# Second-layer sums of one batch moved from VectorE to GpSimd, and the third layer's first loads issued by GpSimd

## The chip, the cores and the metric

The kernel runs on one core of a Trainium2 chip. The metric is the time on the device in microseconds. TensorE is called PE, VectorE DVE, ScalarE ACT, GpSimd POOL, and SyncE, which issues most DMAs, SP.

## What is computed

The input x is 2 x 256 x 64 x 64 in float32 and passes through four layers:

```python
# layer 0: attention
xn = group_norm(x);  q, k, v = split(einsum(xn, w_qkv))        # 4 heads of 64, 4096 pixels
x = xn + w_proj @ (softmax(q k^T / 8) v) + b_proj
# layer 1: x = x + pe, a fixed position term
# layer 2: bottleneck with a deformable 3x3 convolution on 64 channels
h = relu(bn1(w1 @ x))
off = conv3x3(h, woff) + boff                                  # 9 x (dy, dx) and 9 masks
samp = bilinear(h, base + off) * sigmoid(mask)                 # four corners, weighed and summed
x = relu(bn3(w3 @ relu(bn2(einsum(samp, w2) + b2))) + x)
# layer 3: twice group norm, relu, deformable 3x3 convolution on 256 channels
f = depthwise7x7(h, dw);  off = pw @ f + pwb                   # offsets
h = einsum(bilinear(h, base + off), w) + b
out = h + x
```

## The kernel before

**Order.** `attention` (layers 0 and 1, and most of layer 2 in its background) is followed by `deform` (layer 3, with the second batch's layer-2 convolution in its background). PE, ACT, DVE and POOL execute in the order in which the program issues their instructions; the order of SP's DMAs is left to the scheduler of the framework.

**Attention.** There are four units (batch, pair of heads), each of 16 blocks of 256 queries, each of 16 score tiles of 128 x 1024. The loop takes two tiles at a time, a pair: PE makes scores (L538), DVE their maxima (L547), ACT the exponentials (L554), PE transposes them (L566), DVE or ACT copies the transposes (L581, L583), and PE multiplies by the values (L593). DVE copies the product to `o` (L432). At the end of a block the factors of its parts go through DRAM (`share_d`) into `f`, and POOL combines (L477, L478, L483, in some blocks L485); seven slots later PE projects (L502).

**Background.** Beside its own planned steps, a pair has up to three slots in which generators do a step each. The first batch's `before` (image of h, offsets, corners) runs beside unit 1, its `conv` beside units 2 and 3, then `early_image`, which writes the normalized result to DRAM `xn_d[0]`. The second batch's `before` ends after the last block.

**The convolution of layer 2.** `conv` has 144 steps a batch. A step gathers two corner tiles of 128 x 256 by indirect DMA from POOL (L775), four steps ahead in attention; DVE weighs them by the corner weights in place (L956, "weigh"); one background step later it adds corners pairwise (L965) and once more (L966, "add"), which gives two sampled taps. Four such sums form a group, which PE transposes (L976) after the next sum has been issued, or at once for the last group; there are 40 groups. PE then multiplies (L985, L994). The gather buffers (`bfour`) are five in attention, nine in `deform`.

**Memory.** Tile pools lie in SBUF in the order in which they are opened. In `attention`, `att_w`, `att_work` and `att_one` are opened first, so they lie lowest; `att_one` holds `o`, `f`, `res`, `avs` and others that are used until attention's last instructions. In `deform` the pool `df_w` is opened first, over the same addresses; it holds `x0` (32 KB a partition), `wide0`, `wide1`, `dw`, `pw`, `wf` and nine weights `wc0` to `wc8`.

**The start of layer 3.** `load(0, ...)` reads `xn_d[0]` into `x0` by four DMAs of 1 MB on SP (L1122); POOL clears `wide` (L1127); `offset_weights` reads `dw` and `pw` on SP (L1133, L1135) and DVE makes `wf` of them (L1140); nine `wc` are loaded on SP (L1154). PE then computes offsets (L735, L752, L766), DVE their corners (L680 to L718), and POOL gathers (`four`, L775). `Side` makes a generator keep a rate of steps; before the main loop, 58 rounds advance the first offsets by two steps and the second batch's `conv` by one in every three rounds:

```python
offs = [Side(-LEAD - 6, OFFS / BLOCK, offsets(0, 0))]
for k in range(K2):
    conv_weight(0, k)
for s in range(-LEAD - 6, 0):
    offs[0].follow(s + 1)
    if s % 3 == 0:
        next(second)
```

Of the kernel before, what the change touches and what calls it, by code (L numbers as in the profile page):

```python
# [9 lines left out]
F32 = mybir.dt.float32  # L10
# [8 lines left out]
P = 128  # L19
B, C, H, W = 2, 256, 64, 64  # L20
# [5 lines left out]
DWK = 7  # L26
# [12 lines left out]
class Net:  # L39
# [108 lines left out]
    def attention(self, bott):  # L148
# [4 lines left out]
        tc, nc, a = self.tc, self.nc, self.a  # L153
        with ExitStack() as ctx:
            wp = ctx.enter_context(tc.tile_pool(name="att_w", bufs=1))
            work = ctx.enter_context(tc.tile_pool(name="att_work", bufs=2))
            one = ctx.enter_context(tc.tile_pool(name="att_one", bufs=1))
            xp = ctx.enter_context(tc.tile_pool(name="att_x", bufs=4))
            qp = ctx.enter_context(tc.tile_pool(name="att_q", bufs=2))
            kp = ctx.enter_context(tc.tile_pool(name="att_k", bufs=5))  # L160
            vp = ctx.enter_context(tc.tile_pool(name="att_v", bufs=6))
            ep = ctx.enter_context(tc.tile_pool(name="att_e", bufs=4))
            etp = ctx.enter_context(tc.tile_pool(name="att_et", bufs=2))
            bt = bott.pools(ctx)
            psc = ctx.enter_context(tc.tile_pool(name="att_sc", bufs=2, space=PSUM))
            ptp = ctx.enter_context(tc.tile_pool(name="att_tt", bufs=2, space=PSUM))
# [30 lines left out]
            for i in range(NB):  # L197
                t = xp.tile([P, 2, 512], F32, name="xb") if i < 4 else rest[:, i - 4]
# [8 lines left out]
            gmask = wp.tile([P, P], F32, name="gmask")  # L207
            nc.sync.dma_start(gmask, a["gmask"][:, 0, :])
            nc.sync.dma_start(wqkv, a["wqkv"])
            wproj = wp.tile([P, 2, C], F32, name="wproj")  # L210
            self.later.append((wproj, a["wproj"]))

            units = [(b, hp) for b in range(B) for hp in range(2)]
# [415 lines left out]
            n = 0  # L629
# [153 lines left out]
    class Bottleneck:  # L783
# [148 lines left out]
        def conv(self, b, pools, ps):  # L932
            net, nc = self.net, self.net.nc
            s, t = net.bn_s, net.bn_t
# [15 lines left out]
            def weigh(n):  # L950

                i, g, js = steps[n]
                four, ks = fours.pop(n), self.GROUPS[g]
                w = self.w4[b, i]
                w = w[:, js[0], ks[0] : ks[0] + 2, :] if g < 4 else w[:, js[0] : js[0] + 2, ks[0], :]
                nc.vector.tensor_tensor(  # L956
                    four, four, w.unsqueeze(3).to_broadcast([P, 2, 4, CM]), ALU.mult
                )
                return four

            def add(n, four, sampled):

                i, g, js = steps[n]
                sm = pools["s"].tile([P, 2, CM], F32, name="bsmp")
                nc.vector.tensor_add(four[:, :, 0:2, :], four[:, :, 0:2, :], four[:, :, 2:4, :])  # L965
                nc.vector.tensor_add(sm, four[:, :, 0, :], four[:, :, 1, :])  # L966
                if g < 4:
                    sampled.append(sm.rearrange("p n f -> p (n f)"))
                else:
                    sampled.extend(sm[:, m, :] for m in range(2))  # L970
# [41 lines left out]
            for n, (i, g, js) in enumerate(steps):  # L1012
                gather(n + ahead)
                if g == 0 and js == (0,):
                    x = self.block(pools["x"], net.xa_d[b], i)
                four = weigh(n)
                yield "b"
                add(n, four, sampled)
                if last:
                    last.popleft()()  # L1020
# [63 lines left out]
    def deform(self, bott):  # L1084
# [4 lines left out]
        tc, nc, a = self.tc, self.nc, self.a  # L1089
        with ExitStack() as ctx:  # L1090
            wp = ctx.enter_context(tc.tile_pool(name="df_w", bufs=1))
            work = ctx.enter_context(tc.tile_pool(name="df_work", bufs=2))
# [22 lines left out]
            x, stats = {}, dict(bott.stats)  # L1115

            def load(b, src, pool):
                x[b] = pool.tile([P, 2, HW], F32, name=f"x{b}")
                src = src.rearrange("(cb p) n -> p cb n", p=P)
                for i in range(4):  # L1120
                    cols = slice(1024 * i, 1024 * i + 1024)
                    nc.sync.dma_start(x[b][:, :, cols], src[:, :, cols])  # L1122

            load(0, self.xn_d[0], wp)
            ods = [wp.tile([P, 8, W + DWK - 1], F32, name=f"wide{n}") for n in range(2)]
            for t in ods:
                nc.gpsimd.memset(t, 0.0)  # L1127
            base = bott.base

            def offset_weights(l):  # L1130

                dw = wp.tile([P, 2, T], F32, name="dw")
                nc.sync.dma_start(dw, a["dw"][l])  # L1133
                pw = wp.tile([P, 2, 2 * K2], F32, name="pw")
                nc.sync.dma_start(pw, a["pw"][l])  # L1135
                yield
                yield
                self.wf = wp.tile([P, 2, T, 2 * K2], F32, name="wf")
                for cb in range(2):
                    nc.vector.tensor_tensor(  # L1140
                        self.wf[:, cb],
                        dw[:, cb].unsqueeze(2).to_broadcast([P, T, 2 * K2]),
                        pw[:, cb].unsqueeze(1).to_broadcast([P, T, 2 * K2]),
                        ALU.mult,
                    )
                    yield
# [9 lines left out]
            def image(b, l):  # L1156

                if l == 0:
                    load(b, self.x2d[b], ctx.enter_context(tc.tile_pool(name="df_x1", bufs=1)))
# [39 lines left out]
            def offsets(b, l):  # L1199
                if b == 0:  # L1200
                    yield from offset_weights(l)
                wf = self.wf
                for i in range(NB):
                    idx = cp.tile([P, 4, K2], I32, name="didx")
                    w4 = cp.tile([P, 4, K2, 4], F32, name="dw4")
                    corners[b, l, i] = idx, w4
                    yield from self.offsets(
                        i,
                        [x[b][:, cb, :] for cb in range(2)],
                        lambda s, row: wf[:, s, DWK * row : DWK * row + DWK, :].rearrange(  # L1210
                            "p t o -> p (t o)"
                        ),
                        self.vec[:, V_PWB + l : V_PWB + l + 1],
                        base, idx, w4, work, ods, pd,
                    )

            layers = [(b, l) for l in range(2) for b in range(B)]
            BLOCK = 4 * K2
            LAYER, ALL = NB * BLOCK, len(layers) * NB * BLOCK
            AHEAD, LEAD = 8, BLOCK + 16  # L1220
# [119 lines left out]
            OFFS = 24  # L1340
            inner = ExitStack()
            second = bott.conv(1, bott.pools(inner, 9), ps)
            offs = [Side(-LEAD - 6, OFFS / BLOCK, offsets(0, 0))]
            for k in range(K2):
                conv_weight(0, k)
            for s in range(-LEAD - 6, 0):
# [10 lines left out]
            for s in range(ALL + 12):  # L1357
                n = s // LAYER
# [22 lines left out]
                if s % LAYER == LAYER - LEAD - 8 and n + 1 < len(layers):  # L1381
                    for o in images + offs:
                        for _ in o.steps or ():
                            pass
                    images, offs = [], []
                    offs.append(Side(s, OFFS / BLOCK, offsets(*layers[n + 1])))
# [97 lines left out]
```

## Time and profile before

| what | value |
|---|---|
| median of 3 runs | 5523.4 us (5519.6 to 5540.4) |
| profiled execution | 5528.8 us, span 5527.0 us |
| PE busy | 4928.5 us (89%) |
| DVE busy | 4232.0 us (77%) |
| ACT busy | 2888.5 us (52%) |
| POOL busy | 2069.2 us (37%) |
| POOL's DMA queue | 679.59 MB; SP's 234.46 MB |

Attention ends at about 3100 us of the span, the second batch's `conv` at about 3900 us, and the third layer fills the rest. A line of the timeline gives start, length, engine, program line, operation, tile written and tile read; a number in square brackets is how long the engine had been idle, and behind it what released it. "SPq" and "POOLq" are the sequencers that issue DMAs. A group's line gives the count, then busy us and mean ns, then idle us before and their releasers. Issue instructions are not counted as busy time.

### The profile page before, as it was taken

To read this page: it belongs to the slowest core of one execution; us is meant where nothing else is said; L and a number is where in the kernel's file an instruction comes from. 1 tells how busy PE (TensorE), PEld (TensorE's weight loads), DVE (VectorE), ACT (ScalarE), POOL (GpSimd) and SP (SyncE) were. 2 spreads that over 40 slices of the span, in tenths; PEclk is the share of its full clock that TensorE was granted. 3 is DMA by queue.
4 is the path that set the end of the run, shared out by engine and by line. 5 is a ranking of instruction groups with operands and counts; after the bars stand their busy time and mean duration, and the time that the engine had idled before them with its cause. 6 is when DMAs were issued, how large, how long until landed. Compare 5 with 4: busy or idle time off the path is not lost.

```text
span 5527.0 us, 99087 instructions
## 1 busy us (share of the span) xinstructions
PE 4928.5 (89%) x37976; PEld 2677.3 (48%) x37976; DVE 4232.0 (77%) x8066; ACT 2888.5 (52%) x5333; POOL 2069.2 (37%) x1947
## 2 busy tenths in 40 slices
PE   8999999999999998999899746555899999999998
PEld 5555555555555555555555322222444444444443
DVE  6878767777588787578566366657798989999998
ACT  5676656666566666566667312122444444444444
POOL 0111110100034333232000266656466556656665
PEclk9999999999999999999999878777999999999999
DMA  5231111111222222222411366655999999999998
GB/s 164 65 93 47 51 57 49 34 43 34 63 68 83 86 83 83 85 70 61 132 46 28 108 209 198 186 182 187 330 322 331 329 333 348 345 389 349 337 349 305
DMA packets 347369, 920.38 MB, mean 167 GB/s; under 512 B 58972, under 2 KB 98698, under 8 KB 346894
## 3 DMA queue, kind: packets, MB, share of 16 engines
q0 software_dynamic: 193536, 679.59, 35.4%
q1 hardware_dynamic: 153358, 234.46, 13.8%
q8 instruction: 298, 4.88, 0.4%
q14 instruction: 177, 1.45, 0.1%
HBM read 815.90 MB, written 89.60 MB: 164 GB/s over the span
## 4 chain that ended last, share of the span: by engine, by line
PE 64%; DVE 16%; issue 8%; ACT 6%; another core or an unknown queue 4%; DMA 1%; POOL 1%; ACTq 0%; SPq 0%; DVEq 0%; POOLq 0%
PE av L593 14%; PE sc L538 14%; PE out L1285 10%; PE tt L566 9%; DVE smp L1254 8%; PE pd L735 5%; PE pt L1266 3%; DVE low L547 2%; ACT e L554 2%; DVE bfour L956 1%; PE pm L985 1%; DVE bfour L965 1%; PE pm L502 1%; PE pm L249 1%
## 5 line engine op out<-in xcount | busy, mean ns | idle before, releaser
L1254 DVE SCALAR_TENSOR_TENSOR smp<-four,dw,smp 128x256 f32<-128x256 f32 x3456 | 1612.1, 483 | 311.2 <-ACT smp L1248 162.8
L554 ACT ACTIVATE e<-sc,low 128x1024 f32<-128x1024 f32 x1024 | 1146.0, 1119 | 734.4 <-DVE low L547 714.1
L775 POOL DMA_INDIRECT four<-img,didx x1152 | 1159.1, 1006 | 738.1 <-DVE smp L1254 299.1
L547 DVE TENSOR_REDUCE low<-sc 128x1 f32<-128x1024 f32 x1024 | 1209.4, 1219 | 282.4 <-PE sc L538 273.2
L1285 PE MATMUL out<-st,wc 128*128 128x512 f32 x2304 | 1238.5, 620 | 199.5 <-ACT st L1275 114.9
L538 PE MATMUL sc<-k,qs 64*128 64x512 f32 x2048 | 1026.4, 620 | 10.1 <-ACT e L554 9.5
L538 PE MATMUL sc<-k,q 64*128 64x512 f32 x2048 | 1015.3, 619 | 0.5 <-issue 0.5
L593 PE MATMUL av<-et,v 128*64 128x256 f32 x8192 | 1005.6, 385 | 0.0
L566 PEld LDWEIGHTS tt<-ident,e 64*128 64x128 f32 x16384 | 662.8, 139 | 582.1 <-issue 287.1
L477 POOL TENSOR_TENSOR o<-o,f 128x1024 f32<-128x1024 f32 x64 | 153.1, 2392 | 1934.2 <-DMA f<-share_d 924.7
L775 POOL DMA_INDIRECT bfour<-img,bidx x576 | 581.3, 1009 | 743.6 <-DVE bsmp L966 545.3
L566 PE MATMUL tt<-ident,e 64*128 64x64 f32 x16384 | 731.2, 227 | 96.0 <-ACT et L583 80.3
L583 ACT COPY et<-tt 128x512 f32<-128x512 f32 x1280 | 722.2, 587 | 105.8 <-PE tt L566 80.3
L1275 ACT COPY st<-pt 128x1024 f32<-128x1024 f32 x288 | 291.3, 1012 | 927.6 <-PE pt L1266 637.3
L593 PEld LDWEIGHTS av<-et,v 128*64 128x64 f32 x8192 | 558.3, 137 | 306.7 <-issue 57.8
L1266 PEld LDWEIGHTS pt<-ident,smp 128*128 128x128 f32 x2304 | 321.1, 145 | 771.8 <-issue 503.2
L581 DVE COPY et<-tt 128x512 f32<-128x512 f32 x768 | 525.2, 684 | 171.6 <-PE tt L566 148.3
L1285 PEld LDWEIGHTS out<-st,wc 128*128 128x128 f32 x2304 | 393.4, 197 | 460.2 <-issue 280.0
L1248 ACT ACTIVATE smp<-four,dw 128x256 f32<-128x256 f32 x1152 | 514.2, 502 | 68.1 <-DMA four<-img,didx 55.9
L1266 PE MATMUL pt<-ident,smp 128*128 128x128 f32 x2304 | 459.5, 282 | 93.1 <-DVE smp L1254 80.6
L538 PEld LDWEIGHTS sc<-k,qs 64*128 64x128 f32 x2048 | 349.0, 191 | 263.3 <-issue 133.7
L735 PE MATMUL pd<-x,wf 128*126 128x512 f32 (+2 forms) x896 | 463.0, 604 | 10.1 <-issue 9.2
(154 smaller groups left out, 3342.5 us busy)
## 6 DMA issues: line engine op xcount, KB each, us to landing
f<-share_d SPq DMA_DIRECT2D x128, 256.0 KB
xb<-xn SPq DMA_DIRECT2D x55, 512.0 KB
img<-imgt SPq DMA_DIRECT2D x96, 256.0 KB
four<-img,didx POOLq DMA_INDIRECT x1152
xa<-res SPq DMA_DIRECT2D x32, 512.0 KB
xb<-in_x SPq DMA_DIRECT2D x20, 512.0 KB
bfour<-img,bidx POOLq DMA_INDIRECT x576
qs<-q SPq DMA_DIRECT2D x64, 128.0 KB
```

What stands on the lines that cost most here:

```text
L538: nc.tensor.matmul(s[:, j, :], lhsT=q[u, i // 2][int(h != j)][halves[j], at : at + P], rhs=k[u][c][halves[j], h, :], start=True, stop=True,)
L547: nc.vector.tensor_reduce(low, s, AX.X, ALU.max, negate=True)
L554: nc.scalar.activation(e.rearrange("p j n -> p (j n)"), s, AF.Exp, bias=blk.low[:, g, c : c + 1], accum_out=blk.sum[:, g, c : c + 1],)
L566: nc.tensor.transpose(pt[:, m, :], e[half, m // 4, m % 4 * P : m % 4 * P + P], self.ident[half, half],)
L581: nc.vector.tensor_copy(dst, pt)
L583: nc.scalar.copy(dst, pt)
L593: nc.tensor.matmul(now["av"][halves[h], :], lhsT=v[u][c][:, m, halves[h]], rhs=ets[j][:, m, h, :], start=(m == 0), stop=(m == 7),)
L735: nc.tensor.matmul(pd[:m, r0 * W : r1 * W], lhsT=wt(s, t), rhs=src[:, (y + r0) * W : (y + r1) * W], start=(n == 0), stop=(n == len(srcs) * ...
L775: self.nc.gpsimd.indirect_dma_start(out=dst, out_offset=None, in_=img, in_offset=bass.IndirectOffsetOnAxis(ap=idx, axis=0),)
L1254: nc.vector.scalar_tensor_tensor(smps[s], four[:, c], weight(s, c), smps[s], ALU.mult, ALU.add)
L1266: nc.tensor.transpose(pts[u][:, c, j * P : (j + 1) * P], smp[:, c * P : c * P + P], self.ident,)
L1285: nc.tensor.matmul(outs[ob], lhsT=wc[k][:, c, ob * P : ob * P + P], rhs=sts[u][:, c, :], start=(k == 0 and c == 0), stop=(k == K2 - 1 and ...
```

## The change

- In `attention` the pools `att_work` and `att_one` are opened after the larger ones and so lie above them; `wproj` moves from `att_w` into `att_one`.
- In `conv`, both adds of the first batch go to POOL; those of the second batch stay on DVE. The weighing stays on DVE for both.
- In `deform`, the loads of x of the first batch, and the first layer's `dw` and `pw`, are issued by POOL and no longer by SP.
- The generator of the first offsets is begun (its first step, the two loads) before x is loaded and `wide` is cleared; `Side` receives it with one step done.

```diff
             wp = ctx.enter_context(tc.tile_pool(name="att_w", bufs=1))
-            work = ctx.enter_context(tc.tile_pool(name="att_work", bufs=2))
-            one = ctx.enter_context(tc.tile_pool(name="att_one", bufs=1))
...
             etp = ctx.enter_context(tc.tile_pool(name="att_et", bufs=2))
+            work = ctx.enter_context(tc.tile_pool(name="att_work", bufs=2))
+            one = ctx.enter_context(tc.tile_pool(name="att_one", bufs=1))
...
-            wproj = wp.tile([P, 2, C], F32, name="wproj")
+            wproj = one.tile([P, 2, C], F32, name="wproj")
...
                 i, g, js = steps[n]
+                engine = (nc.gpsimd, nc.vector)[b]
                 sm = pools["s"].tile([P, 2, CM], F32, name="bsmp")
-                nc.vector.tensor_add(four[:, :, 0:2, :], four[:, :, 0:2, :], four[:, :, 2:4, :])
-                nc.vector.tensor_add(sm, four[:, :, 0, :], four[:, :, 1, :])
+                engine.tensor_add(four[:, :, 0:2, :], four[:, :, 0:2, :], four[:, :, 2:4, :])
+                engine.tensor_add(sm, four[:, :, 0, :], four[:, :, 1, :])
...
-                    nc.sync.dma_start(x[b][:, :, cols], src[:, :, cols])
-
-            load(0, self.xn_d[0], wp)
-            ods = [wp.tile([P, 8, W + DWK - 1], F32, name=f"wide{n}") for n in range(2)]
-            for t in ods:
-                nc.gpsimd.memset(t, 0.0)
+                    queue = (nc.gpsimd, nc.sync)[b]
+                    queue.dma_start(x[b][:, :, cols], src[:, :, cols])
...
+                queue = (nc.gpsimd, nc.sync)[l]
                 dw = wp.tile([P, 2, T], F32, name="dw")
-                nc.sync.dma_start(dw, a["dw"][l])
+                queue.dma_start(dw, a["dw"][l])
                 pw = wp.tile([P, 2, 2 * K2], F32, name="pw")
-                nc.sync.dma_start(pw, a["pw"][l])
+                queue.dma_start(pw, a["pw"][l])
...
+            begun = offsets(0, 0)
+            next(begun)
+            load(0, self.xn_d[0], wp)
+            ods = [wp.tile([P, 8, W + DWK - 1], F32, name=f"wide{n}") for n in range(2)]
+            for t in ods:
+                nc.gpsimd.memset(t, 0.0)
...
-            offs = [Side(-LEAD - 6, OFFS / BLOCK, offsets(0, 0))]
+            offs = [Side(-LEAD - 6, OFFS / BLOCK, begun)]
```

## The prediction

> **What bounds the kernel now.** I read the slices of the page first: PE is 9 tenths busy in the first 22 slices (attention) and the last 12 (third layer), and 5 to 7 tenths between about 3100 and 3900 us. The change touches two places: the first batch's second layer, which runs inside attention, and the handover from attention to the third layer. So I asked for windows. The first row below is attention without this work, the others are attention with it (columns: window, length, then busy us and instructions of PE, PEld, DVE, ACT, POOL, then PE clock, DMA share, GB/s).
>
> ```profile
> 800.00:1440.00 640.00, 632.92 (x6880) 375.68 (x6880) 483.92 (x746) 411.08 (x765) 65.38 (x45) 1.00 0.15 42
> 1612.00:2240.00 628.00, 579.80 (x5923) 336.41 (x5920) 488.67 (x742) 400.23 (x744) 253.92 (x225) 0.98 0.29 84
> 2330.00:2626.00 296.00, 276.05 (x2850) 162.02 (x2850) 235.68 (x370) 197.23 (x369) 97.45 (x88) 0.99 0.25 71
> ```
>
> PE idles 7.1 us of 640 (1.1%) in the first, 48.2 + 20.0 = 68.2 us of 924 (7.4%) in the others. At 1.1% it would idle 10; so **58 us is all that these windows can give back**. In the chain of waits the first window is PE (618 us) with 20 us of ACT; in the other two PE is 572 us and DVE 197, of which the moved sums are 44 (L965 24.3 + 10.5, L966 4.3 + 5.3). The reason: scores feed the maximum (L547, DVE), that feeds the exponential, that feeds PE's transposes; a sum ahead of L547 in DVE's order delays all three. From the groups of instructions, 1580 to 2626 us, the rows concerned:
>
> ```profile
> L547 DVE TENSOR_REDUCE low<-sc 128x1 f32<-128x1024 f32 x328 | 387.8, 1218 | 123.5 <-PE sc L538 118.8 <-remote 2.6 <-PE tt L566 0.2
> L956 DVE TENSOR_TENSOR bfour<-bfour,bw 128x512 f32<-128x512 f32 x144 | 101.8, 707 | 0.4 <-issue 0.4
> L965 DVE TENSOR_TENSOR bfour<-bfour 128x256 f32<-128x256 f32 x144 | 81.5, 566 | 1.7
> L966 DVE TENSOR_TENSOR bsmp<-bfour 128x128 f32<-128x128 f32 x144 | 58.7, 408 | 4.9
> L775 POOL DMA_INDIRECT bfour<-img,bidx x280 | 276.0, 986 | 547.3 <-DVE bsmp L966 485.5 <-issue 49.7 <-DVE lowest L436 6.1
> L477 POOL TENSOR_TENSOR o<-o,f 128x1024 f32<-128x1024 f32 x20 | 49.1, 2455 | 84.1 <-DVE o L432 43.3 <-DVE pos L689 29.4 <-DVE bsmp L966 5.6
> ```
>
> The last two columns are busy and mean, then the idle before. POOL has room: it idles 485 us before gathers, waiting for the sums to free a buffer. The medians of L965 and L966 are 419 and 292 ns, so their means hold 21 + 17 = 38 us of stall. The timeline shows where from:
>
> ```profile
> 1916.12 2.67 POOL L477 TENSOR_TENSOR o<-o,f 128x1024 f32<-128x1024 f32 x1 [3.12 <-DVE o L432]
> 1916.61 2.46 DVE L965 TENSOR_TENSOR bfour<-bfour 128x256 f32<-128x256 f32 x1
> ```
>
> A sum of 0.42 us takes 2.46, until POOL's multiply has ended.
>
> At the handover the timeline reads (start, length, engine, line):
>
> ```profile
> 3105.13 0.72 POOL L483 TENSOR_TENSOR avs<-o 128x256 f32<-128x256 f32 x1
> ...
> 3115.24 0.37 SPq L1122 DMA_DIRECT2D x<-xn  x1
> ...
> 3122.45 0.99 POOL L775 DMA_INDIRECT bfour<-img,bidx  x1 [6.07 <-ACT bod L904]
> ...
> 3135.01 0.34 SPq L1133 DMA_DIRECT2D dw<-in_dw  x1
> ...
> 3136.14 0.34 SPq L1135 DMA_DIRECT2D pw<-in_pw  x1
> ...
> 3143.03 2.07 DVE L1140 TENSOR_TENSOR wf<-dw,pw 128x882 f32<-128x882 f32 x2 [4.07 <-DMA pw<-in_pw]
> ...
> 3144.17 13.73 PE L735 MATMUL pd<-x,wf 128*126 128x512 f32 x28 [9.25 <-issue]
> ```
>
> The first load of x goes when attention's tail frees its place; dw and pw go last on SP, behind nine weights; DVE waits 4.07 us for pw, and PE's first offsets follow.
>
> **What the Trainium skill says.** "SBUF — State Buffer", "Who interferes with whom": a DVE instruction with two SBUF inputs and a GpSimd one that reads SBUF exclude each other, and the later waits; the pair of rows above agrees (2.46 against 0.42 us). "GPSIMD Engine Reference", "3.1 Elementwise": a two-input add costs about 2.6 cycles an element at 1.2 GHz; the undisturbed L477, L478 and L483 (2357, 1273, 729 ns for 1024, 512, 256 elements, window 783 to 1456) give 2.12 ns an element, which is that. "DMA: Bandwidth & Descriptors", "SWDGE vs HWDGE vs iDMA": descriptors of a DMA issued from GpSimd are made by its own cores; the trace of before has only POOL's gathers to show it, 0.95 us and 0.30 between.
>
> **The sums.** DVE loses 144 x (0.42 + 0.29) = 102 us and their 38 us of stalls. On POOL a sum of 256 elements costs 0.73 (L483's row) and one of 128 an estimated 0.46 (the 256 one less 128 x 2.12 ns): 1.19, with gaps 1.27 a step, 144 x 1.27 = 183 us. POOL then does 276 + 280 x 0.30 = 360 us of gathers, 116 of the attention's combining (L477, L478, L483, L485) and 183: 659 of 1046, 63%. It is not full. The wait of a gather for the sums of four steps before stays as it was, only within POOL.
>
> Gain: the chain bounds it at 44 us to first order, PE's idle time at 58, and zero is the other end (another late term could take over at once). New against it: the weighing (L956, two SBUF inputs, still DVE) meets POOL reading 171 + 116 = 287 us of 1046, 27% of the time; 144 x 0.27 x about 0.6 us, half of a POOL operation, is 23 us of stall where 4 are now. DVE's moved time was on the chain for 44 of 140 us, 0.31; 19 x 0.31 = 6. That leaves 38 by the chain and 52 by the idle time. To choose, I compare DVE with PE where background steps come in bursts, three in a pair of score tiles, that is 1.5 weighings with their sums. The pair itself costs DVE 2 x 1.22 (L547) + 0.68 (L581) + 0.21 (half an L432) = 3.33 us. With the sums a burst adds 1.5 x (0.71 + 0.57 + 0.41) = 2.5, total 5.9 against the 5.0 us of a pair in row one (40.0 us a block of eight): DVE sets the pace. Without them it adds 1.5 x 0.85 = 1.3, total 4.6: PE does. So I take the middle, **45 us**.
>
> Loss: behind a sum on POOL stand the next gathers; for it waits the transpose of four sums (L976), which holds up all of PE. Before, the end of the last L966 to its L976 was 3.6 us in the median of 40 groups, and under 0.5 in nine. I laid POOL's order on the timeline of before: each step two gathers of 1.28 us, then the sums, not before their weighing has ended, and combining (4.4 us, 6.8 with L485) where it stands now. Sums would end a median of 0.4 us later than now, 4.6 later in the worst tenth, mostly behind combining. Eight groups reach L976 late, by 0.3 to 6.2 us, together **20 us**. Two ends: 8, if a late start is made up in the next stall, and 40, if a faster DVE and PE shrink all slack. Second layer and early image end at 2810 and attention at 3100, so a slower background costs nothing else; its cover is 290 us. Projection (L502) stands seven slots after combining, some 17 us, which covers a lag of 5.
>
> **The handover.** Placing the short-lived pools above frees the third layer's first bytes before the tail. POOL issues dw, pw and four loads of x after L483 ends at 3105.9, ahead of two memsets (1.07 us) and the gathers, which go at 3122.45 whatever comes, since they read the image whose last writes SP starts at 3117.22. Six issues have 16.6 - 1.1 = 15.5 us. Price: 0.4 each by SP's row, or 1.25 for dw and pw and 2.5 for an x load of twice a gather's rows: 2.4 to 12.5 us. Hidden at both ends; if an x load took over 3.3, gathers would be late, but the second buffer round waits for DVE anyhow. SP loses those six and issues the nine weights sooner. Then wf need not wait for pw: DVE's previous work, corners of the last block, ends at 3139.0, so wf starts 4.0 us earlier, and PE's offsets (PE free at 3135), their corners at 3162.5 and what waits for these follow. Since the offsets begin one step ahead, the second weighing of batch 1 falls behind the corners (L680), and gather ten waits for its sums: 1.3 us back. Net **-3 us**; ends -6 (DMA less crowded than its 337 to 355 GB/s between 3120 and 3140) and +6 (slow issues). wproj's new pool and the addresses cost nothing: no instruction is added.
>
> **Sum.** 45 - 20 + 3 = 28 us. The profiled execution took 5528.8 us (span 5527.0 and 1.8 around it), which is 5.4 above the median: 5500.8 on its own scale, 5495.4 on that of the runs, which lies on the line of 0.5%, 28 us, about what a measurement of this kernel can tell from no change.
>
> **Rivals.** *PE recovers wholly* (20%): windows two and three come near the first: 58 - 8 + 3 = 53, about 5470. For it: DVE, 78% busy in row two, falls to some 65%, under the 76% of row one, where PE idled 1.1%. Against: the sums behind combining on POOL. *POOL's latency wins* (slower, 15%): price, the mean lateness of the 40 groups; with 48 us gained, the kernel is over 0.5% slower once it exceeds (48 + 28) / 40 = 1.9 us, against 0.5 worked out. If 25 come 4.5 us late, one combining: 112 - 48 = +64, about 5587; at 1.9 it is +28. For it: slack under 0.5 us in nine groups, and bursts in which POOL's 1.5 x 3.9 us exceed a pair. Against: eight late groups, not 25. *The change doesn't do what it says* (10%): DVE's time was only in the chain's way by turns, or slow issues eat the handover: the sum is -5 to +30, about 5528.
>
> **How the numbers follow.** Forecast case 55%: its own range is -45 to -5, and the middle lies on the line, so faster .25, same .30. Recovery: faster .20. Latency: slower .15. The last: same .07, slower .03. Faster 0.45, same 0.37, slower 0.18. The low end takes relief 58, lateness 8 and handover 6 (-56, 5467); the high end relief 20, lateness 40 and handover +6 (+26, 5549); what is beyond is most of the latency case.
>
> **What would show it.** L965 and L966 split: 144 each on POOL between 1580 and 2626, near 0.73 and 0.46 us; PE idle of the two windows down from 68 to about 43; PE waiting for POOL at L976, some 20 us; L956's mean at about 0.8. dw issued near 3106, wf at about 3139, the first `four` gather near 3172 in place of 3175.4, less what attention gained. It is wrong if attention's end moves by under 5 us or over 50, if PE waits for POOL over 50 us, or if the time from attention's last o (3099.1) to the end, 2428 us now, changes by more than 10.

## The result and the profile after

| | before | after |
|---|---|---|
| median of 14 runs each, same chip | 5527.4 us (5515.5 to 5540.4) | 5511.9 us (5494.9 to 5519.1) |
| ratio | | 0.9969, 95% interval 0.9958 to 0.9979 |
| profiled span | 5527.0 us | 5515.6 us |

The changed kernel is 15.5 us faster in the medians, 11.4 in the profiled executions. The prediction said 28. The lines of the code after have moved: L502 is L503, L538 is L539, L547 is L548, L566 is L567, L735 is L736, L956 is L957, L965 and L966 are L967 and L968, L976 is L978, L1122 is L1125.

The two windows in which attention carries the second layer, in the profile after (columns as in the prediction):

```profile
1612.00:2240.00 628.00, 586.57 (x5999) 338.28 (x5998) 425.91 (x565) 405.14 (x752) 366.00 (x405) 0.97 0.28 85
2330.00:2626.00 296.00, 278.53 (x2795) 161.02 (x2793) 205.74 (x283) 194.38 (x361) 144.34 (x164) 0.97 0.23 68
```

DVE has lost 63 and 30 us, POOL has gained 112 and 47, as intended. PE's idle time is 41.4 + 17.5 = 58.9 us; it was 68.2, and 43 was predicted. So most of the relief is missing. The groups of instructions (1580 to 2640 us) show that the operations cost what was said:

```profile
L957 DVE TENSOR_TENSOR bfour<-bfour,bw 128x512 f32<-128x512 f32 x144 | 125.4, 874 | 0.0
L967 POOL TENSOR_TENSOR bfour<-bfour 128x256 f32<-128x256 f32 x144 | 113.4, 787 | 295.3 <-DVE bfour L957 232.9 <-PE pm L978 21.8 <-PE tt L567 20.8
L968 POOL TENSOR_TENSOR bsmp<-bfour 128x128 f32<-128x128 f32 x144 | 70.1, 486 | 11.3
```

The medians of L967 and L968 are 732 and 455 ns, against 0.73 and 0.46 predicted; the weighing's mean rose from 707 to 874 ns, 24 us over 144 of them, against 19. The waits of PE in the same stretch (total us, times, longest) show where the time went:

```profile
PE pm L978 <- POOL bsmp L968: 43.3, 20, 3.5
PE tt L567 <- ACT et L584: 13.7, 21, 3.3
```

The wait for the copied transposes, 47.5 us before, is down to 13.7: that is the relief. A new wait of 43.3 us, for POOL's second sum, takes its place. Two of its 20 instances in the timeline (the number after the start is the length; PEld's idle time is given, PE's own is 1.9 and 3.5):

```profile
2074.49 2.96 DVE L957 TENSOR_TENSOR bfour<-bfour,bw 128x512 f32<-128x512 f32 x1
2074.53 2.36 POOL L478 TENSOR_TENSOR o<-o,f 128x1024 f32<-128x1024 f32 x1
...
2079.35 2.35 POOL L486 TENSOR_TENSOR res<-res,pos 128x1024 f32<-128x1024 f32 x1
...
2081.66 1.17 POOL L967 TENSOR_TENSOR bfour<-bfour 128x256 f32<-128x256 f32 x1
2082.91 0.45 POOL L968 TENSOR_TENSOR bsmp<-bfour 128x128 f32<-128x128 f32 x1
2083.41 0.14 PEld L978 LDWEIGHTS pm<-ident,bsmp 128*128 128x128 f32 x1 [2.17 <-POOL bsmp L968]
...
2086.70 0.45 POOL L968 TENSOR_TENSOR bsmp<-bfour 128x128 f32<-128x128 f32 x1
2087.21 0.18 PEld L978 LDWEIGHTS pm<-ident,bsmp 128*128 128x128 f32 x1 [3.65 <-POOL bsmp L968]
...
2087.61 1.22 PE L539 MATMUL sc<-k,q 64*128 64x512 f32 x1
```

POOL combines a block until 2081.7 and only then makes the sums that PE wants. PE waits twice, once for each of two steps of POOL, which lie 3.8 us apart (two gathers and two sums). The weighing at 2074.49 takes 2.96 us beside POOL's multiply (L478), where 0.7 is usual; that agrees with the exclusion of "SBUF — State Buffer", "Who interferes with whom", in the Trainium skill. And after the wait a score matmul takes 1.22 us where it takes 0.65 otherwise: PE runs at half its clock. The clock records show 68 us of half clock between 1500 and 2640, against 44 before. The Trainium skill, "TensorE: Matmul & The Clock Gate", "Part 1: The HAM clock gate", says that an idle window of about 3.4 us halves the clock until a busy one has passed. The records here agree in the pieces, 3.4 and 6.8 us long, but shorter waits suffice: after the ones of 1.7 us at 2407 and 2.2 us at 1929 the clock is halved too.

At the handover the timeline after reads:

```profile
3087.82 0.60 POOL L1133 DMA_DIRECT2D dw<-in_dw  x1 [34.53 <-PE av L594]
3088.42 0.57 POOL L1135 DMA_DIRECT2D pw<-in_pw  x1
3088.97 0.74 POOL L1125 DMA_DIRECT2D x<-xn  x1
3089.76 2.34 POOL L478 TENSOR_TENSOR o<-o,f 128x1024 f32<-128x1024 f32 x1
...
3092.89 3.68 DVE L1140 TENSOR_TENSOR wf<-dw,pw 128x882 f32<-128x882 f32 x2 [5.24 <-DMA pw<-in_pw]
...
3094.78 0.85 POOL L484 TENSOR_TENSOR avs<-o 128x256 f32<-128x256 f32 x1
...
3098.37 7.66 PE L736 MATMUL pd<-x,wf 128*126 128x512 f32 x12 [11.18 <-DMA x<-xn]
3105.95 1.08 PE L503 MATMUL pm<-avs,wproj 128*64 128x512 f32 x4
...
3119.31 1.03 POOL L776 DMA_INDIRECT bfour<-img,bidx  x1 [21.92 <-DMA img<-imgt]
```

The loads are issued among attention's last combining steps, not behind them, and the third layer's first products (L736) stand ahead of attention's last projection (L503). This has a price. PE waits for the load of x, then makes 7.7 us of these products, and the projection begins 10.3 us after its input `avs` is done. Before, it began at once:

```profile
3105.90 1.98 PE L502 MATMUL pm<-avs,wproj 128*64 128x512 f32 x4 [7.27 <-POOL avs L483]
```

So the projection comes at the same time as before, although attention ends 11.4 us earlier, and the second batch's first gather, at 3119.3 in place of 3122.5, gains only 3.1 us of them. In all nine profiles with the changed handover the projection waits in this way, 8 to 10 us; in the five with the handover of before it doesn't (0.05 us).

**Chips.** The experiments ran on several chips, on which the kernel before takes 5323, 5523 and 5600 us, so ratios are always to the kernel before on the same chip. They are called the 5323, the 5523 and the 5600 chip; the runs above (5527) are like the 5523 one, and the last experiment ran on a second chip of the 5323 kind (5322). "Attention's end" is the start of the last block's `lowest` on DVE (L436), which closes the scores of the last block (3088.3 us in the profile before, 3076.9 after). It is read from one profile of each kernel.

### The profile page after: what moved, and what is told of

Read it like the earlier page. It is cut to its first block, busy times and chain, and to the rows that moved or that the text cites. A ratio compares the mean times of both kernels' runs of the same rounds, so it can differ in the third digit from the quotient of the medians.

```text
span 5515.6 us, 99167 instructions
## 1 busy us (share of the span) xinstructions
PE 4938.5 (90%) x37976; PEld 2674.7 (48%) x37976; DVE 4129.4 (75%) x7778; ACT 2889.7 (52%) x5333; POOL 2245.7 (41%) x2241
## 4 chain that ended last, share of the span: by engine, by line
PE 63%; DVE 13%; issue 7%; another core or an unknown queue 5%; POOL 5%; ACT 5%; DMA 2%; SPq 0%; ACTq 0%; POOLq 0%; DVEq 0%
PE av L594 14%; PE sc L539 13%; PE out L1292 10%; PE tt L567 9%; DVE smp L1261 7%; PE pd L736 5%; PE pt L1273 3%; POOL bfour L776 2%; ACT e L555 1%; PE pm L250 1%; PE pm L987 1%; PE pm L503 1%; DMA four<-img,didx 1%; ACT smp L1255 1%
## 5 line engine op out<-in xcount | busy, mean ns | idle before, releaser
L548 DVE TENSOR_REDUCE low<-sc 128x1 f32<-128x1024 f32 x1024 | 1209.4, 1219 | 380.1 <-PE sc L539 367.7
L539 PE MATMUL sc<-k,qs 64*128 64x512 f32 x2048 | 1029.4, 621 | 7.1 <-ACT e L555 6.5
L539 PE MATMUL sc<-k,q 64*128 64x512 f32 x2048 | 1015.0, 620 | 0.0
L567 PEld LDWEIGHTS tt<-ident,e 64*128 64x128 f32 x16384 | 661.3, 140 | 535.8 <-issue 274.1
L478 POOL TENSOR_TENSOR o<-o,f 128x1024 f32<-128x1024 f32 x64 | 152.4, 2381 | 1864.4 <-DVE o L433 779.6
L567 PE MATMUL tt<-ident,e 64*128 64x64 f32 x16384 | 731.1, 227 | 49.5 <-ACT et L584 45.5
L736 PE MATMUL pd<-x,wf 128*126 128x512 f32 (+2 forms) x896 | 469.9, 611 | 16.8 <-DMA x<-xn 11.2
L539 PEld LDWEIGHTS sc<-k,qs 64*128 64x128 f32 x2048 | 350.4, 192 | 248.2 <-issue 125.5
```

Of the source, the lines that this page charges most:

```text
L539: nc.tensor.matmul(s[:, j, :], lhsT=q[u, i // 2][int(h != j)][halves[j], at : at + P], rhs=k[u][c][halves[j], h, :], start=True, stop=True,)
L548: nc.vector.tensor_reduce(low, s, AX.X, ALU.max, negate=True)
L567: nc.tensor.transpose(pt[:, m, :], e[half, m // 4, m % 4 * P : m % 4 * P + P], self.ident[half, half],)
L736: nc.tensor.matmul(pd[:m, r0 * W : r1 * W], lhsT=wt(s, t), rhs=src[:, (y + r0) * W : (y + r1) * W], start=(n == 0), stop=(n == len(srcs) * ...
```

## The experiments

### Each half alone (5323 chip)

My theory was the one of the prediction, with the new wait as its loss; the rival, that the loads give the gain and the sums none.

`e1_sums_only` is the kernel before with `engine = (nc.gpsimd, nc.vector)[b]` in `add`; `e2_loads_only` is the changed kernel with

```diff
-                engine = (nc.gpsimd, nc.vector)[b]
                 sm = pools["s"].tile([P, 2, CM], F32, name="bsmp")
-                engine.tensor_add(four[:, :, 0:2, :], four[:, :, 0:2, :], four[:, :, 2:4, :])
-                engine.tensor_add(sm, four[:, :, 0, :], four[:, :, 1, :])
+                nc.vector.tensor_add(four[:, :, 0:2, :], four[:, :, 0:2, :], four[:, :, 2:4, :])
+                nc.vector.tensor_add(sm, four[:, :, 0, :], four[:, :, 1, :])
```

> The kernel before with only the first batch's sums on GpSimd; pools and loads as before. Theory (relief and lateness): attention ends about 11 us earlier, as in the changed kernel (last maximum of the last block 3076.9 against 3088.3), PE waits some 43 us for POOL at the transposes of the sums, and the time falls by 8 to 14 us, ratio about 0.998. Rival (the handover makes the whole gain, and the attention's 11 us are given back later): ratio 0.9995 to 1.0005.

> The changed kernel with the first batch's sums back on VectorE; pools, GpSimd's loads and the order of the first offsets as in the changed kernel. Theory: attention ends where it did before (3088 us), the first four gather comes about 5 us sooner than before, and the time falls by 3 to 6 us, ratio about 0.999. Rival (the handover makes the whole gain): ratio 0.997, 16 us.

Measured: sums alone 1.0041 (1.0028 to 1.0055), slower, which neither theory nor rival had; loads alone 0.9990 (0.9983 to 0.9996), 5 us, as the theory had it. Attention's end: 3068.1 with the sums moved, 3051.0 without. PE's wait in the first, and the one that it replaces in the second:

```profile
PE pm L977 <- POOL bsmp L967: 44.5, 20, 3.5
```

```profile
PE tt L567 <- ACT et L584: 43.8, 34, 3.0
```

So on this chip the sums cost 17 us in attention: one wait is exchanged for another of its size, with more half clock after it. The whole change would come to 1.0041 x 0.9990 = 1.003 here, if the two parts add up; it was not run on this chip.

### The late sums taken out in two ways (5323 chip)

`e3_sums_unread` lets POOL make the sums, and PE turns a constant in their place, so no wait for a sum can be left (the result then lacks the first batch's sampled values). `e4_late_turn` keeps everything and turns a group one sum later than the changed kernel does, the last group of a block two background steps later.

```diff
+                    if b == 0:
+                        sm = net.ident            # e3, in transpose
```

```diff
-                    last.popleft()()
+                    due, turn = last.popleft()
+                    if b == 1 or n >= due:
+                        turn()
+                    else:
+                        last.appendleft((due, turn))
...
-                last.append(lambda g=g, sm=sampled: sts.append(transpose(g, sm)))
+                last.append((n + 2, lambda g=g, sm=sampled: sts.append(transpose(g, sm))))
...
-                    last.popleft()()
+                    for _ in range(2 * (b == 0)):
+                        yield "any"
+                    while last:
+                        last.popleft()[1]()
```

> The changed kernel, but the transposes of the first batch's sums read the constant identity in place of the sums, so that PE waits for no sum; the sums are still made on GpSimd (the first batch's sampled values are left out of the result). Theory (lateness takes back what relief gives): PE's 43 us of waiting vanish and attention ends 30 to 43 us earlier than in the changed kernel, ratio to before 0.989 to 0.992. Rival (PE's wait only stands where another wait would come anyway, relief itself is small): attention ends within 10 us of the changed kernel's, ratio 0.996.

> The changed kernel with the transposes of the first batch's groups placed one sum later in PE's order (for the last group of a block two background steps later), same work. Theory: a sum is later than it was by a median of 0.4 us and by 4.6 in the worst tenth, and one step more is 3 us or more of slack, so PE's wait for POOL falls from 43 us to under 12 and attention ends 20 to 35 us earlier than in the changed kernel, ratio to before 0.991 to 0.994. Rival (relief small): within 8 us of the changed kernel, ratio 0.996 to 0.998.

Measured: 0.9905 (0.9890 to 0.9920) and 0.9918 (0.9904 to 0.9931). Attention's end 3009.3 and 3020.6. Against loads alone (3051.0) the relief is **42 us**; against sums alone (3068.1) the lateness is **59 us**. PE's clock accounts for 59 instead of 44.5: half clock lasts 63.2 us in e1 and 34.1 in e3 (1500 to 2640 us), and half of the difference, an estimate of the work lost, is 15; 44.5 + 15 = 60. In `e4_late_turn` the wait is nearly gone:

```profile
PE pm L978 <- POOL bsmp L968: 6.7, 4, 2.5
```

So the theory held here: late sums take the gain. But 42 - 59 = -17 says that the change should be slower, and on the chip of the result it was faster. Something was missing.

### The same on the 5523 chip

Is the gain real there, and does leaving out the sums altogether give the relief? (Loads alone were not run on this chip.) `e5_changed_again` and `e6_before_again` are unaltered. `e7_no_sums` is the kernel before without the first batch's sums on any engine, PE turning a constant in their place; `e8_late_vector` is `e4_late_turn` with the sums on DVE.

```diff
+                if b == 0:                        # e7, in add
+                    sampled.extend([net.ident] * (1 if g < 4 else 2))
+                    return
```

> The changed kernel, unaltered, on the chip of this set. Theory: the sign of the sums' part hangs on how much relief there is, and that differs between chips: sums alone cost 0.41% and the loads alone brought 0.10% where the kernel before took 5323 us; there the two together must give about 1.003. Rival: the gain of 0.31% that was measured at 5527 us holds wherever it runs, and sums without loads are slow for a reason that the loads take away.

> The kernel before, unaltered, for its profile on the chip of this set. Theory: attention's last maximum comes at 3050 to 3060 us where the run takes about 5323 us (as with the sums on VectorE and the new loads, 3051), and at 3088 only on a chip on which it takes 5527; PE's busy share in 1612 to 2240 us is then 95%, not 92%. Rival: it is 3085 to 3091 on every chip and the new pools and loads made the 3051.

> The kernel before, with the first batch's sums left out altogether and its transposes reading the constant identity (the first batch's sampled values are left out of the result). Measures the relief by itself, without locks from POOL's sums. Theory: attention ends 42 to 55 us earlier than in the kernel before, ratio about 0.990 to 0.992. Rival (relief is small): under 15 us, ratio 0.997 or more.

> The changed kernel's pools and loads, the sums on VectorE, and the first batch's transposes one sum later, as in the run with late turns. Theory: most of the late turns' gain is what POOL's sums need; with sums on VectorE PE hardly waited for them (some 2 to 5 us), so ratio 0.996 to 1.000. Rival (the later place helps PE by itself): ratio 0.993 or less, as with the sums on GpSimd.

Measured: the change again 0.9985 (0.9976 to 0.9994); no sums **1.0033** (1.0016 to 1.0050), slower with less work; late turns with DVE's sums 0.9973 (0.9961 to 0.9985). Attention's end: before 3089.2, changed 3082.8, no sums 3100.4, late turns on DVE 3084.3. The gain is there, small. But late turns with the sums left on DVE, 18 us faster than before, are no slower than the changed kernel, and only 4.9 us of their gain lie in attention; where the rest comes from is open. That a kernel without 288 DVE instructions is slower was expected by no theory of mine.

The trace of `e7_no_sums` shows ACT and DVE waiting for PE where PE's own records have the work done. Around one such pause, rows of PE, POOL, ACT and DVE:

```profile
1987.70 0.71 PE L566 MATMUL tt<-ident,e 64*128 64x64 f32 x16
1988.02 0.95 POOL L775 DMA_INDIRECT bfour<-img,bidx  x1 [0.30 <-issue]
...
1988.73 0.59 PE L538 MATMUL sc<-k,q 64*128 64x512 f32 x1
...
1989.27 0.95 POOL L775 DMA_INDIRECT bfour<-img,bidx  x1 [0.30 <-issue]
1990.52 0.94 POOL L775 DMA_INDIRECT bfour<-img,bidx  x1 [0.30 <-issue]
...
1992.34 1.22 PE L538 MATMUL sc<-k,qs 64*128 64x512 f32 x1 [3.01 <-issue]
...
1994.28 0.95 POOL L775 DMA_INDIRECT bfour<-img,bidx  x1 [0.30 <-issue]
1997.01 1.07 ACT L583 COPY et<-tt 128x512 f32<-128x512 f32 x2 [4.72 <-remote]
1997.10 1.23 DVE L547 TENSOR_REDUCE low<-sc 128x1 f32<-128x1024 f32 x1 [9.47 <-remote]
...
1997.64 0.37 PE L566 MATMUL tt<-ident,e 64*128 64x64 f32 x1 [3.23 <-ACT et L583]
```

ACT and DVE wait 4.7 and 9.5 us for transposes and scores of PE, and "remote" means that the trace has no releaser close in time. By PE's records the transposes were done at 1988.4 and the scores at 1989.3, some 8 us before these waits end. Either PE's work or its signal comes later than it is recorded; the trace can't tell which. PE itself stands idle for 3.0 us, with no releaser named, and for 3.2 us, until ACT's copy is made. All the while POOL issues gathers back to back. The kernel before has the same, shorter:

```profile
2082.33 0.71 PE L566 MATMUL tt<-ident,e 64*128 64x64 f32 x15 [0.22 <-issue]
...
2083.76 0.94 POOL L775 DMA_INDIRECT bfour<-img,bidx  x1 [0.30 <-issue]
2085.01 0.95 POOL L775 DMA_INDIRECT bfour<-img,bidx  x1 [0.30 <-issue]
2085.81 0.59 ACT L583 COPY et<-tt 128x512 f32<-128x512 f32 x1 [1.82 <-remote]
...
2087.27 0.69 DVE L581 COPY et<-tt 128x512 f32<-128x512 f32 x1 [3.45 <-remote]
```

I counted, between 1590 and 2620 us of every profile, the waits of DVE and ACT over 1.2 us without a releaser (joined where they overlap; they are called pauses), how long PE is idle within them, and the runs of four and more gathers less than 0.6 us apart:

| kernel | chip | long runs of gathers | of these with a pause | pauses, us | PE idle in them, us |
|---|---|---|---|---|---|
| before | that of the result | 19 | 9 | 23.9 | 13.8 |
| e6_before_again | 5523 | 19 | 10 | 25.4 | 14.2 |
| e7_no_sums | 5523 | 24 | 13 | 61.4 | 38.5 |
| e8_late_vector | 5523 | 19 | 6 | 16.3 | 10.5 |
| e11_loads_again (below) | 5600 | 19 | 10 | 25.4 | 19.3 |
| e2_loads_only | 5323 | 18 | 0 | 0 | 0 |
| after, e5 | result's, 5523 | 0 | 0 | 0 | 0 |
| e9, e10 (below) | 5600 | 0 | 0 | 0 | 0 |
| e1, e3, e4; e12 (below) | 5323, two chips | 0 | 0 | 0 | 0 |

Every pause lies at a long run of gathers or begins within 0.2 us of its end, although these runs fill only 11% of the stretch in the kernel before. With POOL's sums in the queue a run never exceeds two, since two sums follow each pair; the profile after:

```profile
1988.30 0.45 POOL L968 TENSOR_TENSOR bsmp<-bfour 128x128 f32<-128x128 f32 x1
1989.02 0.96 POOL L776 DMA_INDIRECT bfour<-img,bidx  x1 [0.27 <-POOL bsmp L968]
1990.29 0.95 POOL L776 DMA_INDIRECT bfour<-img,bidx  x1 [0.30 <-issue]
1991.26 0.73 POOL L967 TENSOR_TENSOR bfour<-bfour 128x256 f32<-128x256 f32 x1
```

If the long runs cause the pauses, this is a second gain of the moved sums, on the chips with pauses only: an estimated 14 us by PE's idle time in them, 24 by their whole length. It would also account for `e7_no_sums`. Without sums the runs are longer (13 of five and more, against 7). The pauses grow by 24 us (PE's idle time) or 36 (whole length), and half clock lasts 95.6 us where before has 47.8 on this chip, which costs half of the difference, 24. Less the 39 us of relief without its clock part, that is 9 to 21 us later at attention's end; measured were 11.2.

### The 5600 chip

Three edits were repeated on another chip; the rival was that pauses fill in whatever wait is removed.

> The same edit as e4_late_turn: the whole change, with TensorE's turning of a group's sums put off by two more steps. Theory (the wait of TensorE for GpSimd's second sum, 43 us in the profile after, is what took the gain on the chip of the first measurement too): with the wait gone some 43 us come off the 5512 of the changed kernel; ratio to the kernel before 0.989 to 0.992, attention's end near 3035. Rival (on the slower chip other pauses of TensorE, which the trace doesn't explain, take the place of any wait that is removed): ratio 0.995 to 0.998, attention's end 3065 or later, although the wait for GpSimd is below 10 us. If the chip is of the faster kind, 0.992 as in e4_late_turn.

> The same edit as e3_sums_unread: the whole change, with GpSimd's sums made as in it, and TensorE turning the constant identity in their place for the first batch (so the second layer's sampled values of that batch are left out of the result). It differs from e9_late_again only in that no wait for a sum can be left. Theory: 0.988 to 0.991, as e9_late_again or up to 6 us below it. Rival (unexplained pauses fill what is freed): 0.995 to 0.998. On the faster kind of chip 0.9905.

> The same edit as e2_loads_only: the whole change with the first batch's sums left on VectorE, so that only the third layer's first loads are issued by GpSimd. Theory (the handover is worth 3 to 5 us wherever it runs): ratio 0.999, within 0.9975 to 1.0005. Rival (on the slower chip the loads gave the whole of the changed kernel's 8 to 16 us and the sums nothing): 0.997.

Measured: 0.9829 (0.9806 to 0.9853), 0.9814 (0.9791 to 0.9837) and 0.9939 (0.9918 to 0.9961): all three gains larger than theory or rival had. Against loads alone on this chip, late turns are 0.989 and unread sums 0.987, about what the theory had against the kernel before. Attention's end: 3027.3, 3021.3 and 3101.4. The two windows of late turns, then of loads alone:

```profile
1612.00:2240.00 628.00, 610.97 (x6419) 357.94 (x6417) 436.30 (x585) 427.10 (x794) 355.37 (x393) 1.00 0.29 88
2330.00:2626.00 296.00, 280.77 (x2807) 162.31 (x2806) 208.74 (x302) 197.28 (x367) 133.66 (x150) 0.97 0.23 67
```

```profile
1612.00:2240.00 628.00, 577.16 (x5915) 336.97 (x5914) 489.20 (x747) 400.07 (x747) 250.42 (x223) 0.98 0.29 85
2330.00:2626.00 296.00, 273.12 (x2774) 160.55 (x2770) 230.67 (x362) 191.90 (x358) 98.66 (x90) 0.97 0.25 72
```

PE idles 32 us in the first and 74 in the second. Between `e11` and `e10` lie 80 us at attention's end. From the other chip's relief (42 us, of which 3 are half clock), this chip's pauses (19 by PE's idle time, 25 by length) and half of the difference in half clock (54.6 - 30.7 = 23.9, so 12) I estimate 70 to 76. That fits both gains being realised here, relief and pauses, and the rival falls. The 0.9939 of loads alone, 34 us, is not explained: no profile of the kernel before was taken on this chip, and the handover gave it only some 5 us (86.4 us from attention's end to the third layer's first sampled product, 91.0 in the profile before). It is larger than the whole gain of the changed kernel on the chip of the result. So how the total there splits between sums and loads is not shown; the profiles show only that attention ends earlier.

### The runs of gathers broken up by themselves

This was to show the pauses' cause directly: DVE keeps its sums, and memsets that compute nothing part the gathers.

```diff
                 nc.vector.tensor_add(sm, four[:, :, 0, :], four[:, :, 1, :])
+                for _ in range(2 * (b == 0)):
+                    nc.gpsimd.memset(four, 0.0)
```

> The kernel before, with VectorE's sums left where they are, and two GpSimd memsets (0.53 us each by the row of the same shape in the profile before) into the gathered buffer once its sums are made: they compute nothing, and keep more than two gathers of the first batch from being issued back to back. Theory (TensorE's unexplained pauses come where GpSimd issues four and more gathers in a row; the profiles that keep to pairs, all of them with sums on GpSimd, have none): on a chip that shows the pauses (before near 5523 or 5600) the DVE and ACT waits of over 1.2 us that the trace puts down to nothing fall from 17 to at most 3, attention's end comes 25 to 40 us earlier (24 us of pauses in the profile before, and the half-speed clock after them), ratio 0.993 to 0.996. Rival (the pauses vanish because VectorE is relieved of its sums, and the length of the bursts goes with that by chance): the pauses stay, attention's end within 8 us of before or later, ratio 0.9985 to 1.002. On the faster kind of chip (before near 5323), which shows no pauses, both expect 0.999 to 1.002.

It ran on the second chip of the 5323 kind, on which no pauses were expected: 1.0007 (0.9999 to 1.0015). Runs longer than two are gone (135 pairs, five single ones), and the 288 memsets cost about 4 us, 8 at the end of the interval, although POOL spends 152.5 us on them:

```profile
L968 POOL MEMSET bfour<- 128x512 f32 x288 | 152.5, 529 | 325.1 <-DVE bsmp L966 316.8
```

So the price of parting the gathers is known, its gain on a chip with pauses is not. Attention ends at 3042.2 here, with the pools and loads of before; so the earlier end on this kind of chip (3051.0 in e2, against 3088 to 3089 on the slower ones) is not the work of the new pools and loads, the rival of `e6_before_again`. That it is 9 us earlier than in e2, on another chip, leaves room for a small part of the 42 us of relief to be due to the parted gathers. That runs of gathers cause the pauses therefore rests on their coincidence in the profiles of the slower chips, and on the kernels there in which both are gone with the sums on POOL. How a gather could hold up PE or its signals, and why only on some chips, stays open.

## Why the prediction was right, and where not

**The bound and the relief: right.** PE's idle time in the two windows was what could be won, and DVE's sums were the cause of most of it. 45 us were predicted, 42 measured on the 5323 chip; on the chip of the result the relief was not measured by itself.

**The prices: right.** 1.19 us a step on POOL, the same in the medians; the weighing's stall 24 us where 19 were said.

**The lateness: the step that failed.** Its term was 20 us, from eight late groups; the profile shows 20 waits in 16 of the 40 groups and 43.3 us, just over the upper bound of 40. The working laid POOL's order on the timeline of before, in which DVE and PE still had their stalls. Two things moved. Counted from a group's last weighing, PE is free for the group's transposes after 4.9 us in the median, where it was 5.8 before; and the group's last sum ends after 3.7 us in the median and 9.2 in the worst tenth, where it was 2.7 and 5.5. The upper bound had named the first ("if a faster DVE and PE shrink all slack"); it should have been the middle value. What the term lacked wholly is what a wait does to PE's clock: on the 5323 chip 44.5 us of wait cost 59.

**A term that was not in the sum.** The pauses in the profile before, 23.9 us, were in the views that I read (the wait of PE for copied transposes, rows with "remote"), and I counted all of PE's idle time as DVE's doing. With the moved sums the gathers are parted, and the pauses are gone. An estimate for the chip of the result: relief 39 without its clock part, pauses 14 (PE's idle time in them) to 24, wait -43, and half of the half clock's growth, (68 - 44) / 2 = -12, come to between -2 and 8 us; measured at attention's end 11.4, and 6.4 in the second pair of profiles. If this account is right, the total fell inside the range by luck: a loss that was twice too small met a gain that was left out. On the 5323 chip, without that gain, the rival "POOL's latency wins" is what e1 shows: its point was a mean lateness of (48 + 28) / 40 = 1.9 us for over 0.5% slower; 59 / 40 = 1.5 gave 0.41%.

**The handover: the size about right, the path wrong.** -3 us was predicted. The first sampled product of the third layer came 16.4 us earlier, attention's end 11.4: -5.0, and -4.7 in the second pair. But dw went at 3087.8 and wf at 3092.9, not at 3106 and 3139. The section on the kernel before says that the engines execute in the order in which the program issues instructions, and I built on this; the profile after shows that it does not hold across the handover, since POOL's L1133 and PE's L736 stand before attention's L478 and L503. So the gathers of the second batch did not go "at 3122.45 whatever comes" either: counted from attention's end they went 8 us later than before, behind the projection that L736 held up. The price of an x load from POOL, bounded by 0.4 and 2.5 us, was 0.72 to 0.76; dw and pw took 0.60 and 0.57.

**The rest: right within the scatter.** From attention's end to the kernel's end both profiles take 2438.7 us, so the 5 us of the handover do not reach the end in this pair; in the second pair the stretch is 7.4 us shorter (2438.7 against 2446.1). The second batch's last weighing begins at 3891.1, before at 3888.3, later in spite of the earlier start, and what follows it is 14 us shorter. Two profiles of the kernel before differ by 11 us there (3888.3 and 3899.5), so a few us of this stretch can't be read from single profiles.

**A version that beats both.** Late turns: 0.9918 on the 5323 and 0.9829 on the 5600 chip. The changed kernel ran beside it on neither, but its only measured ratios are 0.9969 and 0.9985, and its parts give 1.003 on the 5323 chip. On the 5600 chip a part of the 0.9829 is the unexplained 0.9939 of loads alone.

## What to carry to other kernels

Work that moves to an idle engine moves its consumer's deadline too: lay the new order on a timeline from which the stalls to be removed are already gone, and give the consumer slack (one step more sufficed here) in the same edit. Price a wait of TensorE by its length and by the half clock after it. Before idle time is credited to an engine, separate the gaps whose releaser the trace doesn't name, and look what the other queues do in exactly those microseconds. When the next stage's first work is made ready sooner, look whether it now stands ahead of the last stage's work on the same engine.

## What the runs showed of the hardware

- On two kinds of chip VectorE and ScalarE waited 1.3 to 9.5 us for results of TensorE, in 6 to 13 places, at runs of four and more indirect gathers that GpSimd issued 0.3 us apart; in the longest, TensorE's own records had the work done some 8 us before. On the 5323 chip 18 such runs left no pause. The cause is open.
- One kernel took 5323, 5523 and 5600 us on three chips, and the sign of one edit seems to differ between them: the sums and the loads together 1.003 (worked out from 1.0041 and 0.9990) against 0.9969 and 0.9985 (measured).
- TensorE's clock was halved for 3.4 us after waits as short as 1.7 and 2.2 us.
- A 1 MB load issued by GpSimd held its queue 0.72 to 0.76 us, a small one 0.57 to 0.60.
